# FFN of a two-layer DiT block: two elements at a time, first product as seven block products of 256 columns

## The chip, the cores and the metric

The kernel runs on one core of one Trainium2 chip. The metric is the device time of one execution in microseconds (us). A core has a matrix engine (TensorE, PE in the profile; PEld is its weight load), which writes only to PSUM, eight banks of 512 fp32 columns; VectorE (DVE) and ScalarE (ACT), which read and write PSUM and SBUF; GpSimd (POOL), which works on SBUF; and SyncE (SP), which here issues nearly all DMAs. Each engine works through its own queue, and semaphores order the queues.

## The reference

There are sixteen elements of 256 tokens by 256 channels, in fp32. Two layers follow each other; each is self attention, cross attention and a feed-forward network (FFN), every one preceded by a layer norm whose scale and shift are made from a condition vector ("modulation"), and followed by a residual sum. The change touches the two FFNs:

```python
h = _ln(x, ...) * (1 + scale) + shift        # per element, 256 x 256
g = gelu(h @ W1 + b1)                        # W1: 256 x 1024, exact gelu
x = x + g @ W2 + b2                          # W2: 1024 x 256
```

## The kernel before, in words

The work is cut into six phases (layer 0 self attention, cross attention, FFN; the same for layer 1), and each phase into sixteen jobs, one per element b (list `jobs`, from L840 on). A job has two steps in an attention phase and four in an FFN phase. The main loop goes through all steps; what is called in a step is written out by hand for each kind of phase. `manual_schedule` (L86) covers PE, DVE, ACT, POOL and SP: each of these engines executes its instructions in the order in which the program issues them, and there is no planner. In step s of job j the loop also works for neighbours: `prev` is j-1, `nxt` j+1, `after` j+2 and `third` j+3.

The input of a job takes this way. `prepare_moments` (L421) finds mean and variance on DVE and raises the variance to the power -0.5 on POOL. `prepare_norm` (L424) normalizes on DVE, transposes 32x32 blocks on DVE (`turn`, L352), writes them to DRAM with four DMAs on SP (`turned`), and adds the bias of the coming output to x on POOL (`add_bias`, L428). `prepare_fetch` (L444) reads them back transposed with four DMAs on SP (`fetched`). `prepare_input` (L449) applies scale and shift (`affine`, L402): the first 128 channels on ACT, the second on POOL, giving `hT`, channels by tokens, as two 128x256 blocks.

In an FFN job, step s calls `ffn_hidden` (L700): 2 of the 8 chunks of 128 hidden channels, each with two accumulated products over the 256 input channels, and a gelu of each chunk on ACT. `product` (L77) issues a 128x128 weight as four matmuls of 32 columns of the weight; the profile records two matmuls for each of these. So the hidden product of an element is 128 records of 256 columns. The output product of the element before runs in step 2 (`finish_folded`, L747): it is already a two-by-two block product with seven instead of eight multiplications; its operands are sums of blocks, made on DVE at step 0 (`fold_inner`, L738) for the activations and once per phase (`fold_weights`, L723) for the weights. It is 224 records of 128 columns. Five DVE additions then put the seven results into x. PSUM banks for an FFN are taken in rotation (`next_bank`, L73).

In the FFN jobs before the change the loop orders the calls so, beside hidden product and output product: moments and norm of `third` at step 1, fetch of `after` at step 1, input of `after` at step 3. In the first FFN phase three modulations for layer 1 are made: at step 3 of elements 2, 5 and 8 (L976) `modulation_turned` (L200) multiplies on TensorE, copies on ACT, transposes on DVE and issues sixteen small DMAs on SP (`turned_b`, L218); the scale and shift are computed from them at step 3 of elements 3, 6 and 9 (L949). At step 1 of element 3 the next phase's weights are loaded. In the second FFN phase, element 2 starts the load of all softmax sums back into SBUF (`look_outside`), and after step 3 of element 3 `judge` (L796) reduces them on DVE with two 128x2048 reductions.

At the start of an FFN phase the last attention job is still unfinished. In layer 0 its softmax sums are inverted in step 1 of element 0 (`sum_up`, L614, with DMAs on SP), its result is scaled on POOL at step 3 (`scale`, L631), and its output product runs at step 3 of element 1. In layer 1 its sums are inverted in step 0 of element 0 (`normalize`, L686: reciprocal and two shuffles on DVE, DMAs on SP, a multiplication on POOL) and its output product runs at step 2.

Of the kernel before, what the change touches and what calls it, by code (L numbers as in the profile page):

```python
# [10 lines left out]
F32 = mybir.dt.float32  # L11
I32 = mybir.dt.int32
AF = mybir.ActivationFunctionType
# [3 lines left out]
P = 128  # L17
# [26 lines left out]
def fast(ctx: ExitStack, tc: tile.TileContext, a: dict, out: bass.AP, flag):  # L44
# [6 lines left out]
    assert NB >= 11  # L51
# [25 lines left out]
    def product(out, lhsT, rhs, start, stop):  # L77


        for g in range(4):  # L80
            cut = slice(32 * g, 32 * g + 32)
            nc.tensor.matmul(out[cut], lhsT[:, cut], rhs, start=start, stop=stop)  # L82
# [239 lines left out]
    def zero_values():  # L322
        for i in range(2):
            wide_v.append(work.tile([P, NT, 8, 64], F32, tag="v", name=f"wide_v{i}"))
            nc.gpsimd.memset(wide_v[i], 1.0)
# [76 lines left out]
    def affine(pt, cw, scale, bias, tag, name, eng=nc.gpsimd):  # L402

        dst = work.tile([cw, 2, N], F32, tag=tag, name=name)
        nc.scalar.activation(dst[:, 0, :], pt[:, 0, :], AF.Identity, bias=bias(0), scale=scale(0))  # L405
        eng.tensor_scalar(dst[:, 1, :], pt[:, 1, :], scale(1), bias(1), ALU.mult, ALU.add)
        return dst
# [41 lines left out]
    def prepare_input(job):  # L449

        b, key = job["b"], job["key"]
        factor, addend = job["phase"]["mod"]
        job["hT"] = hT = affine(
            job.pop("hraw"), P,
            lambda c: factor[:, c, b : b + 1], lambda c: addend[:, c, b : b + 1], "hT", f"hT_{key}",
            nc.vector if b == 0 and job["p"] == 0 else nc.gpsimd,
        )
        if not job["cross"]:
            job["kT"] = hT
        elif job["layer"] == 0:  # L460
            job["kT"] = affine(
                job.pop("craw"), P,
                lambda c: column("L0_xcond_ca_lnc_w", c), lambda c: column("L0_xcond_ca_lnc_b", c),
                "cT", f"cT_{key}",
            )
# [23 lines left out]
    def layer1_values(job, at, t):  # L489
        w, kT = job["phase"]["w"], job["kT"]  # L490
        if t == 0:
            if not wide_v:
                zero_values()
            job["v"] = wide_v[job["index"] % 2]
# [227 lines left out]

    def fold_weights(ph):  # L723
# [3 lines left out]
        for m, x, y, op in ((1, b[0][0], b[1][1], ALU.add), (3, b[0][1], b[1][1], ALU.subtract),  # L727
                            (4, b[1][0], b[0][0], ALU.subtract), (6, b[0][0], b[0][1], ALU.add),
                            (7, b[1][0], b[1][1], ALU.add)):
            if ph["kind"] == "attn":  # L730
                folded[m] = wtile([P, 4, P], "folded", f"folded_w_{m}", 5)
            elif m == 7:
                folded[m] = work.tile([P, 4, P], F32, tag="cT", name=f"folded_w_{m}")
            else:
                folded[m] = work.tile([P, 4, P], F32, tag="qk", name=f"folded_w_{m}", bufs=4)
            (nc.gpsimd if ph["kind"] == "attn" else nc.vector).tensor_tensor(folded[m], x, y, op)
# [176 lines left out]
    for i, (j, s) in enumerate(steps):  # L913
# [40 lines left out]
        if ffn:  # L954
            ffn_hidden(job, s)
            if s == 1 and prev["kind"] == "attn" and layer0:
                sum_up(prev, next_bank())
            if s == 2 and prev["kind"] == "attn" and not layer0:
                finish(prev, next_bank())
            if prev["kind"] == "ffn":  # L960
                if s == 0:
                    fold_inner(prev, nc.vector, 5, 2, 1, 7, 6)
                if s == 2:
                    finish_folded(prev, (next_bank(), next_bank()))
            then = attention(i + 2, 1)
            if s == 2 and then:
                stage_a(then[0], 0, next_bank())
            if s == 0 and prev["kind"] == "attn" and prev["layer"] == 1:
                normalize(prev)
            if late is not None and s == 3:  # L970
                finish(late, next_bank())
            if s == 2 and then:
                for t in range(NT):
                    layer1_values(then[0], next_bank(), t)
            if make_mod:
                make_mod["mod"] = make_mod["make_mod"](next_bank())  # L976
            if s == 1 and after is not None:
                prepare_fetch(after)
            if s == 1 and third is not None:
                prepare_moments(third)  # L980
                prepare_norm(third)
            if s == 1 and prev["kind"] == "attn":
                fold_weights(job["phase"])
            if s == 3 and after is not None:
                prepare_input(after)
            if s == 3 and prev["kind"] == "attn" and layer0:
                scale(prev)
        elif layer0:
            then = attention(i + 1, 0)
            stage_t(job, 2 * s, 0)  # L990
# [32 lines left out]
            if s == 0:  # L1023
                prepare_moments(third)
                context_moments(third)
                prepare_fetch(after)
            else:
# [5 lines left out]
        else:  # L1033
# [16 lines left out]
            else:  # L1050
                prepare_norm(third)
                prepare_input(after)
        scores(i + 1)
# [4 lines left out]
    fold_inner(jobs[-1], nc.vector, 6, 5, 2, 1, 7)  # L1058
    finish_folded(jobs[-1], (1, 2, 3))
# [615 lines left out]
```

## Time and profile before

Three runs of the kernel took 2192.76 to 2195.17 us.

| | us |
|---|---|
| median of the runs shown | 2192.9 |
| profiled execution | 2193.98 |
| its span | 2192.2 |
| TensorE busy | 2175.6 |
| VectorE busy | 1663.5 |
| GpSimd busy | 1072.9 |
| ScalarE busy | 837.5 |
| first FFN phase, first to last of its matmuls | 1290.2 to 1505.4 |
| second FFN phase | 1974.7 to 2185.7 |

The first group of lines that the prediction shows is from the profile's page: busy time of each engine with its share of the span, busy tenths in 40 equal slices, and the shares of the engines in the chain of work that ended last. The second gives two stretches of the span and the busy time in each. The others are lines of the timeline: start, length, engine (SPq is SP's queue, issuing a DMA), line, operation, tile written and tiles read, shapes, count, and in brackets how long the engine stood idle before it and what ended that. Instructions that follow each other are merged into one line. The matmul ends are modelled, so a busy TensorE says that it had work in flight.

### The profile page before, as it was taken

Reading aid. Unit: us, or ns where it says so; the run is one execution under the profiler, and the core shown is the slowest. Engines: PE = TensorE matmul, PEld = TensorE weight load, DVE = VectorE, ACT = ScalarE, POOL = GpSimd, SP = SyncE. Lnnn points to the kernel's source line nnn. Section 1 sums busy time; section 2 is a strip of 40 time slices with the busy share of each in tenths; the row PEclk is TensorE's granted clock in tenths of the full one; section 3 lists DMA queues with packets and bytes.
Section 4 is the critical chain, followed back from the end, with each engine's and each line's share of the span. In section 5 each row is a group of like instructions: output and inputs, shape, how many; then the busy total and the mean of one; then the engine's idle time right before and its main releaser. Section 6 shows DMA issues by size and latency. Waiting matters only on the chain.

```text
span 2192.2 us, 110839 instructions
## 1 busy us (share of the span) xinstructions
PE 2175.6 (99%) x50504; PEld 1452.2 (66%) x50504; DVE 1663.5 (76%) x3121; ACT 837.5 (38%) x1308; POOL 1072.9 (49%) x1034
## 2 busy tenths in 40 slices
PE   9999999999999999999999999999999999999998
PEld 5656656656666666666666668887665555557898
DVE  6877777776888999989888876564777777777654
ACT  3323323323323332333333332233666666663222
POOL 3766566566657777676776752221322233222220
PEclk9999999999999999999999999999999999999999
DMA  6110110110132221212212033221212232223221
GB/s 192 49 37 23 26 38 23 27 38 22 29 86 69 71 62 35 58 42 45 56 36 61 23 74 87 43 56 27 65 40 42 56 94 57 62 52 86 61 63 37
DMA packets 309320, 117.83 MB, mean 54 GB/s; under 512 B 245652, under 2 KB 292072, under 8 KB 308712
## 3 DMA queue, kind: packets, MB, share of 16 engines
q1 hardware_dynamic: 308296, 110.12, 21.2%
q8 instruction: 397, 6.50, 1.3%
q14 instruction: 83, 0.68, 0.1%
q10 hardware_dynamic: 544, 0.52, 0.1%
HBM read 77.14 MB, written 33.29 MB: 50 GB/s over the span
## 4 chain that ended last, share of the span: by engine, by line
PE 90%; DVE 3%; POOL 2%; DMA 1%; issue 1%; SPq 1%; ACT 0%; DVEq 0%; POOLq 0%; ACTq 0%
PE banks L82 59%; PE banks L578 15%; PE banks L647 9%; PE banks L663 5%; PE banks L514 1%; PE banks L481 1%; DVE m L535 1%; POOL raw L636 1%; POOL qk L543 1%; POOL folded L745 0%; DMA spread<-sums_seen 0%; DMA sums_seen<-inv 0%; SPq L218 0%; DVE squares L605 0%; DVE rows L612 0%
## 5 line engine op out<-in xcount | busy, mean ns | idle before, releaser
L590 ACT ACTIVATE pr<-banks 128x1024 f32<-128x1024 f32 x576 | 487.5, 937 | 414.4 <-PE banks L578 211.0
L543 POOL TENSOR_TENSOR qk<-m,m 128x512 f32<-128x512 f32 x256 | 347.8, 1379 | 298.2 <-DVE m L535 203.9
L535 DVE TENSOR_TENSOR m<-banks,rope 128x512 f32<-128x512 f32 x512 | 324.0, 678 | 83.7 <-POOL qk L543 79.6
L599 DVE TENSOR_TENSOR both<-pr 128x512 f32<-128x512 f32 x256 | 222.3, 882 | 102.8 <-ACT pr L590 102.3
L654 ACT COPY raw<-banks 128x512 f32<-128x512 f32 x128 | 75.2, 587 | 465.7 <-PE banks L647 440.0
L578 PE MATMUL banks<-qk 32*64 32x256 f32 x8192 | 241.3, 378 | 3.6 <-DVE x L762 2.3
L647 PE MATMUL banks<-pr,v 128*32 128x256 f32 x4096 | 233.2, 379 | 0.0
L578 PEld LDWEIGHTS banks<-qk 32*64 32x64 f32 x8192 | 184.6, 131 | 64.4 <-issue 22.8
L713 ACT ACTIVATE g<-banks,cols 128x256 f32<-128x256 f32 x256 | 106.3, 471 | 273.7 <-PE banks L82 262.1
L647 PEld LDWEIGHTS banks<-pr,v 128*32 128x32 f32 x4096 | 132.9, 110 | 88.7 <-ACT pr L590 0.7
L82 PE MATMUL banks<-folded_w,folded 128*32 128x128 f32 x5856 | 177.8, 273 | 0.4 <-issue 0.4
L636 POOL TENSOR_TENSOR raw<-raw,spread 128x512 f32<-128x512 f32 x128 | 163.8, 1313 | 18.3 <-DMA spread<-sums_seen 16.1
L82 PEld LDWEIGHTS banks<-folded_w,folded 128*32 128x32 f32 x5856 | 166.2, 110 | 1.3 <-issue 0.9
L605 DVE STREAM_TRANSPOSE squares<-both 128x1024 f32<-128x1024 f32 x128 | 159.4, 1245 | 4.4
L612 DVE TENSOR_REDUCE rows<-squares 128x32 f32<-128x1024 f32 x128 | 155.4, 1214 | 2.2
L698 POOL TENSOR_TENSOR oT<-oT,spread 128x256 f32<-128x256 f32 x64 | 45.8, 736 | 210.0 <-DVE spread L697 210.0
L339 POOL TENSOR_TENSOR rstd<-ve,neg_half 128x2 f32<-128x2 f32 x95 | 74.3, 782 | 125.4 <-DVE ve L337 122.0
L663 PE MATMUL banks<-pr,wide_v 128*32 128x256 f32 x2048 | 134.4, 379 | 1.1 <-ACT pr L590 1.1
L82 PE MATMUL banks<-hT,wk_sa 128*32 128x256 f32 x2048 | 134.7, 381 | 0.5 <-ACT hT L405 0.5
L432 POOL TENSOR_TENSOR x<-x,bo_b 128x256 f32<-128x256 f32 x96 | 73.1, 782 | 125.9 <-DVE xh L347 125.9
L82 PE MATMUL banks<-hT,wq_ca 128*32 128x256 f32 x2048 | 133.9, 379 | 0.0
L82 PE MATMUL banks<-hT,wq_sa 128*32 128x256 f32 x2048 | 133.9, 379 | 0.0
(167 smaller groups left out, 3693.9 us busy)
## 6 DMA issues: line engine op xcount, KB each, us to landing
turned<-blocks SPq DMA_DIRECT2D x380, 64.0 KB
fetched<-turned SPq DMA_DIRECT2D x380, 64.0 KB
spread<-sums_seen SPq DMA_DIRECT2D x128, 128.0 KB
x<-in_x SPq DMA_DIRECT2D x16, 256.0 KB
fetched_c<-turned_c SPq DMA_DIRECT2D x64, 64.0 KB
cT<-in_ctx_turned SPq DMA_DIRECT2D x16, 256.0 KB
out<-x SPq DMA_DIRECT2D x16, 256.0 KB
ctx<-in_ctx SPq DMA_DIRECT2D x16, 192.0 KB
```

Source lines behind the costliest of these rows:

```text
L82: nc.tensor.matmul(out[cut], lhsT[:, cut], rhs, start=start, stop=stop)
L535: nc.vector.tensor_tensor(m, pq, rope[:, s : s + 1, :].to_broadcast([P, 2, N]), ALU.mult)
L543: nc.gpsimd.tensor_tensor(r, x, y, (ALU.subtract, ALU.add)[out])
L578: nc.tensor.matmul(banks[64 * g : 64 * g + 64, at + h, t * N : (t + 1) * N], lhs, rhs, start=(half == 0), stop=(half == 1 or job["layer"] ...
L590: nc.scalar.activation(pr[:, one], sc[:, one], AF.Exp, scale=0.125 if job["layer"] == 0 else 0.25)
L599: nc.vector.tensor_tensor(job["both"][:, 2 * p : 2 * p + 2, :], pr[:, :, 0, :], pr[:, :, 1, :], ALU.add)
L605: nc.vector.transpose(job["squares"].rearrange("p b k -> p (b k)"), job.pop("both").rearrange("p h n -> p (h n)"))
L612: nc.vector.tensor_reduce(job["rows"][:, u, :], job.pop("squares"), AX.X, ALU.add)
L636: nc.gpsimd.tensor_tensor(part, part, spread[:, u : u + 1, :].to_broadcast([P, 2, N]), ALU.mult)
L647: nc.tensor.matmul(o[32 * h : 32 * h + 32, half, :], v[:, t, col : col + 32], prs[h // 2][:, h % 2, t, :], start=(t == 0), stop=(t == NT - 1),
L663: nc.tensor.matmul(o[32 * h : 32 * h + 32], v[:, t, 4 * c + h, 32 * e : 32 * e + 32], prs[h // 2][:, h % 2, t, :], start=(t == 0), stop=(t ...
L713: nc.scalar.activation(g[:, c, :], ph[:, c, :], AF.Gelu, bias=column(w["b1"], 2 * u + c))
```

## The change

The FFN takes elements 0 to 13 in pairs (2n, 2n+1). The hidden product of a pair is a two-by-two block product: W1 cut into two halves of hidden channels and two of input channels, against the two 128-channel blocks of the two elements, 256 columns each. It is done in a form with seven block products M1 to M7, of which three results are built by adding onto a bank after an engine has read it. Each job does half of the hidden channels of both elements: step 0 issues M1, M6, M5 into three banks, ACT copies M1 out and DVE adds M6 to the copy; step 1 adds M2 onto M1's bank and M7 onto M6's, and DVE makes two more sums; step 2 adds M4 and M3 likewise, and DVE makes the last two. The weight sums are made on POOL before the phase (`fold_input_weights`); the sums of the inputs (`fold_input`) on POOL in step 1 of the odd job before the pair (on DVE for the first pair of the first FFN). The last two elements of each phase keep `ffn_hidden`.

The output product has the same form. Its activation folds move from DVE to POOL (`fold_hidden`) and it runs two jobs late instead of one: two of its seven products in step 1, five in step 3, followed by the additions into x. In the paired jobs the affine of `after` runs wholly on ACT and moves from step 3 to step 1, the fetch from step 1 to step 0, the norm from step 1 to step 2.

```diff
-    def product(out, lhsT, rhs, start, stop):
+    def product(out, lhsT, rhs, start, stop, **more):
...
-            nc.tensor.matmul(out[cut], lhsT[:, cut], rhs, start=start, stop=stop)
+            nc.tensor.matmul(out[cut], lhsT[:, cut], rhs, start=start, stop=stop, **more)
...
-        eng.tensor_scalar(dst[:, 1, :], pt[:, 1, :], scale(1), bias(1), ALU.mult, ALU.add)
+        if eng is nc.scalar:
+            nc.scalar.activation(dst[:, 1, :], pt[:, 1, :], AF.Identity, bias=bias(1), scale=scale(1))
+        else:
+            eng.tensor_scalar(dst[:, 1, :], pt[:, 1, :], scale(1), bias(1), ALU.mult, ALU.add)
...
+    def fold_input(pair, eng):
...
+        eng.tensor_tensor(t1, b[0][1], b[0][0], ALU.subtract)
+        eng.tensor_tensor(t2, b[1][1], t1, ALU.subtract)
+        eng.tensor_tensor(t3, b[1][1], b[0][1], ALU.subtract)
+        eng.tensor_tensor(t4, b[1][0], t2, ALU.subtract)
+        first["inner"] = second["inner"] = {1: b[0][0], 2: b[1][0], 3: b[1][1], 4: t4, 5: t1, 6: t2, 7: t3}
...
+    def block_products(job, out, m, start):
...
+        half = job["b"] % 2
+        for c in range(2):
+            at = (2 * half + c) * P
+            product(
+                out[:, c, :], job["phase"]["input_w"][m][:, at : at + P], job["inner"][m], start and c == 0, True,
+                skip_group_check=True,
+            )
+
+    def pair_hidden(job, pair, part):
...
+            block_products(job, x, 1, True)
+            block_products(job, y, 6, True)
+            block_products(job, z, 5, True)
+            nc.scalar.copy(copy, x)
+            nc.vector.tensor_tensor(six, y, copy, ALU.add)
...
+        if part == 1:
+            block_products(job, x, 2, False)
+            block_products(job, y, 7, False)
+            for c in range(2):
+                gelu(job, top[:, c, :], x[:, c, :], 2 * half + c)
+            nc.vector.tensor_tensor(seven, y, copy, ALU.add)
+            nc.vector.tensor_tensor(bottom2, z, seven, ALU.add)
+        else:
+            block_products(job, y, 4, False)
+            block_products(job, z, 3, False)
+            for c in range(2):
+                gelu(job, bottom2[:, c, :], bottom2[:, c, :], 4 + 2 * half + c)
+            nc.vector.tensor_tensor(bottom, y, copy, ALU.add)
+            nc.vector.tensor_tensor(top2, z, six, ALU.add)
...
-            if prev["kind"] == "ffn":
-                if s == 0:
-                    fold_inner(prev, nc.vector, 5, 2, 1, 7, 6)
-                if s == 2:
-                    finish_folded(prev, (next_bank(), next_bank()))
...
+            if s < 3 and paired:
+                pair_hidden(job, pair, s)
+            elif not paired:
+                ffn_hidden(job, s)
+            if s == 0:
+                if prev["kind"] == "attn" and not layer0:
+                    normalize(prev)
+                if after is not None:
+                    prepare_fetch(after)
+                if done is not None:
+                    fold_hidden(done, nc.gpsimd, 5, 6, 7, 3)
+            if s == 1:
+                if b == 0 and layer0:
+                    sum_up(prev, next_bank())
+                if third is not None:
+                    prepare_moments(third)
+                if done is not None:
+                    output_products(done, 1, 2)
+                if paired and after is not None:
+                    prepare_input(after, nc.scalar)
+                    if b % 2 == 1 and b < NB - 4:
+                        fold_input(jobs[j + 1 : j + 3], nc.gpsimd)
+                if b == 0:
+                    fold_output_weights(job["phase"], nc.vector)
...
+            if s == 2:
+                if third is not None:
+                    prepare_norm(third)
...
+            if s == 3:
+                if done is not None and b < NB - 1:
+                    output_products(done, 4, 5, 6, 7, 3)
+                    add_output(done, 5, 6, 7, 1, 2)
+                if late is not None:
+                    finish(late, next_bank())
+                if make_mod:
+                    make_mod["mod"] = make_mod["make_mod"](next_bank())
...
+            elif leaving and nxt["kind"] == "ffn":
+                prepare_input(after, nc.scalar)
+                fold_input((nxt, after), nc.vector)
+                prepare_norm(third)
...
+                if job["cross"] and job["b"] == 5:
+                    fold_input_weights(phases[job["p"] + 1], nc.gpsimd)
+                if nxt["kind"] == "ffn":
+                    fold_input((nxt, after), nc.gpsimd)
...
-    fold_inner(jobs[-1], nc.vector, 6, 5, 2, 1, 7)
-    finish_folded(jobs[-1], (1, 2, 3))
+    last = jobs[-1]
+    fold_hidden(last, nc.vector, 7, 5, 6, 3)
+    output_products(last, 1, 7, 2, 4, 5, 6, 3)
+    add_output(last, 7, 5, 6, 1, 2)
```

## The prediction, made before the change was run

> **What bounds the kernel now.** I read the busy lines and the 40 slices of the page first, then the chain that ended last, then the timeline of the two FFN phases, which the change rewrites, engine by engine. The busy line, the slices of PE and DVE, and the head of the chain:
>
> ```profile
> PE 2175.6 (99%) x50504; PEld 1452.2 (66%) x50504; DVE 1663.5 (76%) x3121; ACT 837.5 (38%) x1308; POOL 1072.9 (49%) x1034
> PE   9999999999999999999999999999999999999998
> DVE  6877777776888999989888876564777777777654
> PE 90%; DVE 3%; POOL 2%; DMA 1%; issue 1%; SPq 1%; ACT 0%; DVEq 0%; POOLq 0%; ACTq 0%
> ```
>
> TensorE is never idle for a whole slice and is 90% of the chain, so a matmul removed is time removed, and an idle microsecond put into TensorE's stream is a microsecond added. The same by windows: first FFN phase, second FFN phase, and the end of the program (columns: length, busy us of PE, PEld, DVE, ACT, POOL, granted clock, DMA):
>
> ```profile
> 1290.20:1505.40 215.20, 214.83 (x5667) 178.81 (x5659) 132.21 (x328) 61.26 (x145) 57.66 (x72) 1.00 0.28 61
> 1974.70:2185.70 211.00, 210.92 (x5672) 182.52 (x5662) 131.01 (x300) 60.79 (x143) 40.22 (x58) 1.00 0.26 62
> 2188.00:2192.00 4.00, 0.00 (x0) 0.00 (x0) 0.00 (x0) 0.00 (x0) 0.00 (x0) 0.82 0.15 43
> ```
>
> Both phases are full of matmuls. The timeline shows one element's first hidden matmul at 2164.49 and the next at 2177.51, so 13.02 us per element for 128 records of 256 columns and 224 of 128. By columns (61,440) that is 54.3 and 27.1 ns a record.
>
> The waits that matter later are on SP and ACT. In the first FFN phase, timeline of those two engines:
>
> ```profile
> 1332.10 11.54 SPq L218 DMA_DIRECT2D turned_b<-blocks_b  x16
> 1353.72 0.60 ACT L405 ACTIVATE hT<-fetched,add_a,fac_a 128x256 f32<-128x256 f32 x1 [8.69 <-DMA fetched<-turned]
> 1372.33 11.79 SPq L218 DMA_DIRECT2D turned_b<-blocks_b  x16
> 1384.22 1.91 SPq L372 DMA_DIRECT2D fetched<-turned  x4
> 1387.72 0.60 ACT L405 ACTIVATE hT<-fetched,add_a,fac_a 128x256 f32<-128x256 f32 x1 [2.46 <-DMA fetched<-turned]
> 1411.83 12.50 SPq L218 DMA_DIRECT2D turned_b<-blocks_b  x16
> ```
>
> Three times the sixteen small stores of a modulation keep SP for 11.5 to 12.5 us, the next element's fetch is issued right behind them (1384.12, then 1384.22), and ACT stands still until it lands. Today nobody minds: TensorE asks for that ACT result one or two elements later.
>
> **What the skill says.** The Trainium skill, "TensorE: Matmul & The Clock Gate", Architectural detail: ACT and DVE are strict first-in-first-out. The trace agrees: after the 8.69 us above six gelus follow back to back. "DMA: Bandwidth & Descriptors", Anatomy of one DMA: a semaphore wait of a DMA happens on the issuing sequencer. The fetch behind the stores agrees. "PSUM — Partial Sum Buffer", The four PSUM rules: a partial sum may be read, synchronised, in the middle of a group; nothing in this trace does so. "TensorE: Matmul & The Clock Gate" again, What's actually happening: an idle window of about 3.4 us halves the clock and one busy window restores it. The last window above shows a fall, mean 0.82 over 4 us: at half clock that is 1.4 us, so it began some 4.9 us after the last matmul (2185.67).
>
> **The change, part by part.**
>
> *Matmuls removed.* A pair's hidden product had 256 records of 256 columns; fourteen block products of 16 leave 224. 32 x 54.3 ns = 1.74 us per pair, seven pairs, two phases: **-24.3 us**. The output product keeps seven products of 32 records. One block product and one output product each take 0.87 us, so an element becomes 14 x 0.87 = 12.15 us.
>
> *Steady state.* DVE per element: five sums from PSUM (0.69, as the 128x512 row of the residual add: 3.4), moments 1.24, normalizing and turning 1.45, five residual adds 0.42 to 0.69 with their dependences 2.8; total 8.9 to 9.4 of 12.15. POOL: four folds at 1.29 to 1.42 (its rows in attention) 5.4, two bias adds 1.52, a power 0.7, half of the pair's four 128x256 sums at 0.76, 1.5: 9.1. ACT: eight gelus 3.4 (two in 0.84), copy 0.59, both affine halves 1.23: 5.2. All fit behind 12.15; the tightest is the first PSUM sum, which waits for the previous residual adds until about 2.3 us into the element and must be done by 3.5. Cover gone, every late microsecond there is TensorE's. I cost it at 0.
>
> *The new coupling.* The order is what costs. TensorE now adds M2 onto the bank that ACT must copy first, and M7 and M4 onto a bank that DVE must read first. On ACT, the copy of element e+1 is queued behind six gelus of e, and those behind the affine of element e+2, moved from the last step to the second. That affine waits for a fetch on SP.
>
> Ordinary element: the turn ends at 10.3 us, its four stores issue in 2.7 and land 3.1 later (gaps of 3.2 in the trace), the fetch issues in 1.75 and lands 1.7 later: 19.6, which is 7.4 in the next element. Affine 1.2, six gelus 2.6: 11.3; the next copy is due at about 13.0. Covered, with 1.7 us to spare.
>
> *Elements 3, 6, 9 of the first FFN phase.* The sixteen stores start about 2.5 us into them (after the residual adds) and the fetch is queued behind: 2.5 + 11.7 = 14.2, fetch and landing 17.6, affine 18.9, gelus 21.4, copy 22.0. TensorE is through the element at 12.15 plus 0.4 to 0.85 for the modulation. After 6 it needs the copy at 15.4: 6.7 us idle. After 3 and 9 a new pair begins, whose M6 needs t2, that is affine (18.9) and two sums on POOL (1.6): 20.4, where M1 ended at 13.7: 6.7. Three times: **+20.1 us**.
>
> *Entry of the first FFN phase (first matmul 1290.2).* DVE's residual add ends at 1291.5, then come the pair's four sums at 0.42 and the normalizing of element 2. M6 waits 1.5; the first sum and the next then hold M7 0.4 and M4 0.8. Element 2's turn ends at 1294.7 (1292.8 today), its fetch lands at 1303.9, so affine, six gelus and copy end at 18.1 us after entry; TensorE needs that copy at 11.5: 6.9 with signals. Then M4 1.0, and the last attention output waits 1.3 for POOL's scaling, whose sums are also behind that fetch on SP. Sum **+11.9**.
>
> *Entry of the second (1974.7).* The timeline before, DVE and POOL:
>
> ```profile
> 1976.08 1.53 POOL L432 TENSOR_TENSOR x<-x,bo_b 128x256 f32<-128x256 f32 x2 [2.77 <-DVE xh L347]
> 1976.93 1.71 DVE L689 RECIPROCAL sums<-sums 128x256 f32<-128x256 f32 x1
> 1977.59 0.56 POOL L406 TENSOR_SCALAR hT<-fetched,fac_b,add_b 128x256 f32<-128x256 f32 x1
> ```
>
> The pair's sums queue on POOL behind these: 1978.15 + 2 x 0.76 = 1979.7, where M1 ends at 1975.6: 4.15. The reciprocal and two shuffles (2.6) stand before the second PSUM sum: M4 waits 1.7. The fetch of element 2 is behind that reciprocal's stores: copy late by 2.9, M4 by 1.0. Elements 0 and 1 have no output product to fill time, so element 3's affine and the sums of pair (2,3) are late for M6: 5.4. Sum **+15.2**.
>
> *The judging reductions.* Two 128x2048 reductions, 2.28 us each, plus two comparisons, stand on DVE after element 3 of the second phase, between its residual adds and the first PSUM sum of element 4. Spare is 0.5 of 4.9: **+4.4**.
>
> *Small.* The last residual adds after the last product are 0.72 + 0.58 where one of 0.42 stood: **+0.7**. Weight folds: one fewer per FFN; the input folds run on POOL under the last attention products (POOL idles 6.99 us before 1291.9). Value tiles' fill moves within POOL's spare time: 0. Slowed clock: five idles above are longer than 4.9 us, each at most 1.7 us of lost work (half of that page's 3.4, an estimate); 0 to 8.5, I take **+3**.
>
> Sum: -24.3 + 20.1 + 11.9 + 15.2 + 4.4 + 0.7 + 3.0 = **+31.0** on the profiled execution's 2193.98 (span 2192.2): 2225. The median shown is 1.1 lower, so **2224 us**, 1.4% slower. The waits follow from laying rows end to end in queue order and might each be off by a third: 2203 to 2245.
>
> **The rivals.**
>
> *Faster: the affine holds no one.* The fetch is now issued a step earlier, and if it lands before ACT comes to it, M2 finds its copy. Then the 20.1, the 6.9 and 2.9 at the entries and the 5.4 vanish, with the slow clock: 31.0 - 35.3 - 3 = -7.3: **2186 us**. For it: ordinary elements fit by my own count. Against: the three fetches behind sixteen stores are on record. It decides at 28 us of these 35: only if four fifths go is the kernel no slower. 14%.
>
> *Between.* One large group (the modulations, or both entries) is hidden and the rest stays: 2190 to 2203. 8%.
>
> *VectorE becomes the bound.* With POOL folding all through, the 128x512 sums could take 30% longer: 9.4 becomes 12.2, above 12.15, and the first sum comes about 1 us late in each of 28 elements: **2252 us**. Against: with POOL busy in attention, the 128x512 multiplications from PSUM still take 678 ns. 6%.
>
> *The saving does not come.* If weight loads set the pace, fewer columns would buy nothing; but records are dropped whole, load and all, and both shapes run at one rate per column. I give it no share of its own.
>
> **How the numbers follow.** 72% for the likeliest (2203 to 2245; 2224), 8, 14 and 6 for the rest. The range 2190 to 2245 leaves out the faster rival and VectorE's, that is 20%. About 0.2% (4.4 us) is what a measurement of this kernel can tell from no change. Faster takes its rival's 14%, same 4% from the low end of the middle case, slower 82%.
>
> **What would show it.** FFN matmul records fall by 14 x 32 = 448. In the first FFN phase TensorE idles about 6.7 us three times, some 44 us apart, released by ACT's copy or POOL's sum, with ACT waiting for the fetch just before; the phases last 235 and 218 us against 215.2 and 211.0. The prediction is wrong if the affine never waits more than about 4 us in either phase, if M6 of the second phase starts within 1 us of M1's end, or if the elements in between differ from 12.15 us.

## The result and the profile after

The changed kernel takes 2231.7 us (median of four runs, 2230.5 to 2232.9) where the kernel before, run beside it, takes 2192.8 (2191.9 to 2195.2): ratio 1.0176, 95% interval 1.0158 to 1.0193, that is 1.8% slower. The forecast was 2224, slower, with a range to 2245. The profiled execution took 2232.9 us, its span is 2231.1. One execution of the kernel with the stores spread, below, took 4554.2 us and is left out of its times.

From the page of the changed kernel: busy line, slices of TensorE and of its granted clock, shares of the chain that ended last.

```profile
PE 2169.1 (97%) x50056; PEld 1414.1 (63%) x50056; DVE 1682.7 (75%) x3120; ACT 868.8 (39%) x1365; POOL 1238.3 (56%) x1177
PE   9999999999999999999999988799999999998998
PEclk9999999999999999999999999899999999999999
PE 88%; DVE 5%; SPq 2%; POOL 2%; DMA 1%; issue 1%; ACT 1%; DVEq 0%; POOLq 0%; ACTq 0%
```

The saving came as forecast: 50504 - 50056 = 448 records fewer. But TensorE now has four more slices that are not full, three in the first FFN phase (one of them with a lower clock) and one in the second, and busy time fell by 6.5 us only, where 448 records are worth 24.3. Slow matmuls count as busy: part of the saving was paid back in longer records.

The two FFN phases by windows, each from its first matmul to the next phase's first one or the last matmul (columns as in the prediction: length; busy us of PE, PEld, DVE, ACT, POOL; granted clock; DMA). First before, then after:

```profile
1290.18:1499.92 209.74, 209.37 (x5567) 175.11 (x5563) 129.46 (x322) 61.26 (x145) 57.66 (x72) 1.00 0.28 62
1974.74:2185.67 210.93, 210.88 (x5670) 182.52 (x5662) 130.94 (x300) 60.75 (x143) 40.22 (x58) 1.00 0.26 62
```

```profile
1289.40:1528.24 238.84, 207.91 (x5345) 154.61 (x5340) 140.88 (x325) 77.51 (x173) 130.80 (x138) 0.94 0.23 53
2002.64:2223.71 221.07, 205.66 (x5446) 163.80 (x5438) 140.46 (x295) 77.07 (x171) 122.14 (x128) 0.97 0.24 59
```

The first phase is 29.1 us longer, the second 10.1; the attention between them is 474.8 before and 474.4 after, and the end after the last matmul grew from 6.5 to 7.4. With the start of the first FFN 0.8 earlier that is the whole difference of the spans, 38.9. The forecast was 19.8 longer for the first (235 against 215.2) and 7.0 for the second (218 against 211.0).

The waits of TensorE after (what it waited for: us in total, times, longest):

```profile
PE banks L82 <- POOL inner L751: 22.6, 4, 7.8
PE banks L82 <- ACT sums L782: 14.5, 3, 7.2
PE banks L82 <- DVE sums L783: 3.9, 1, 3.9
PE banks L82 <- DVE sums L803: 3.3, 4, 0.9
PE banks L82 <- DVE inner L751: 1.9, 1, 1.9
```

None of these rows was there before. `inner` is a pair's input sum on GpSimd, `sums L782` the copy on ACT, `L783` and `L803` the PSUM sums on VectorE. Together 46.2 us (51.6 forecast). By place, from the timeline: behind the modulations 6.97, 7.17 and 7.76 (21.9), entry of the first phase 1.88, 0.74, 5.59 and 0.81 (9.0), entry of the second 3.88, 0.91, 1.75, 0.81 and 3.99 (11.3), judging 3.94. So the ledger of the two phases is +39.2 = -24.3 + 46.2 + 17.3, and the last term, which my sum had at 3, is worked out below, from one experiment and from the record of the clock.

The queue that I named, in the timelines of ACT and SP after:

```profile
1336.76 11.44 SPq L218 DMA_DIRECT2D turned_b<-blocks_b  x16
1348.30 2.63 SPq L372 DMA_DIRECT2D fetched<-turned  x4
...
1352.60 0.60 ACT L405 ACTIVATE hT<-fetched,add_a,fac_a 128x256 f32<-128x256 f32 x1 [13.35 <-DMA fetched<-turned]
```

and what TensorE does meanwhile:

```profile
1346.86 1.04 PE L82 MATMUL banks<-hT,w_a 128*32 128x256 f32 x16
1354.87 3.64 PE L82 MATMUL banks<-inner,put_w_L_xcond_ff_b 128*32 128x256 f32 x32 [6.97 <-POOL inner L751]
1358.28 1.69 PE L82 MATMUL banks<-hT,w_a 128*32 128x256 f32 x16
1359.80 1.04 PE L82 MATMUL banks<-inner,put_w_L_xcond_ff_b 128*32 128x256 f32 x16
```

The fetch is issued when the sixteen stores are out, ACT stands 13.35 us for it, and block product 6 of element 4 comes 6.97 us after block product 1 is through. Then M6 and M5, two block products, take 3.64 us where a pair of them takes 1.9 elsewhere, and M2 1.69 where it takes 1.04.

### The profile page after: what moved, and what is told of

Same layout as the page of the kernel before. It is cut to its first block, busy times and chain, and to the rows that moved or that the text cites. A ratio compares the mean times of both kernels' runs of the same rounds, so it can differ in the third digit from the quotient of the medians.

```text
span 2231.1 us, 110154 instructions
## 1 busy us (share of the span) xinstructions
PE 2169.1 (97%) x50056; PEld 1414.1 (63%) x50056; DVE 1682.7 (75%) x3120; ACT 868.8 (39%) x1365; POOL 1238.3 (56%) x1177
## 4 chain that ended last, share of the span: by engine, by line
PE 88%; DVE 5%; SPq 2%; POOL 2%; DMA 1%; issue 1%; ACT 1%; DVEq 0%; POOLq 0%; ACTq 0%
PE banks L82 57%; PE banks L582 15%; PE banks L651 9%; PE banks L667 5%; SPq L218 1%; PE banks L518 1%; PE banks L485 1%; DVE m L539 1%; DVE x L868 1%; POOL raw L640 1%; DVE rows L616 0%; DVE both L603 0%; DVE squares L609 0%; DMA fetched<-turned 0%; POOL qk L547 0%
## 5 line engine op out<-in xcount | busy, mean ns | idle before, releaser
L640 POOL TENSOR_TENSOR raw<-raw,spread 128x512 f32<-128x512 f32 x128 | 162.3, 1303 | 21.3 <-DMA spread<-sums_seen 20.1
L868 DVE TENSOR_TENSOR x<-banks,x 128x256 f32<-128x256 f32 (+2 forms) x155 | 82.3, 531 | 68.7 <-PE banks L82 62.1
L582 PE MATMUL banks<-q,k 32*64 32x256 f32 x4096 | 128.3, 381 | 0.4 <-ACT g L717 0.4
L889 POOL TENSOR_TENSOR folded<-raw,raw 128x512 f32<-128x512 f32 x90 | 127.1, 1440 | 2.4
```

The source lines that it names most:

```text
L582: nc.tensor.matmul(banks[64 * g : 64 * g + 64, at + h, t * N : (t + 1) * N], lhs, rhs, start=(half == 0), stop=(half == 1 or job["layer"] ...
L640: nc.gpsimd.tensor_tensor(part, part, spread[:, u : u + 1, :].to_broadcast([P, 2, N]), ALU.mult)
L889: eng.tensor_tensor(folded[m], *sums[m])
```

## The experiments

My theory: fetches and DMAs late on SP hold ACT and GpSimd, and TensorE, whose bank is now added onto, waits for them; the sum of my steps is the loss. The rivals on record: the affine holds no one; VectorE is the bound. A further one came up with the ledger: a clock term several times what I gave it. Each run changes the changed kernel; only the moved factors build on the spread stores, and the last two runs each on the run before. Beside these runs the kernel before took 2193.0 to 2194.3 us, so a difference of 1 to 2 us between two of them tells nothing.

**All hidden products single.** The plain product for all sixteen elements; the new output product, the moved norms and fetches stay. The sums for the pairs fall away too, and the affine goes back to step 3, half of it on GpSimd, because it hangs on the same condition. Do pairs cost what they lost?

```diff
-            paired = b < NB - 2
+            paired = False
```

> All sixteen elements take the plain hidden product (eight products), everything else of the change stays: output product in the new form, two elements late, folds on GpSimd, norm and fetch moved. TensorE gets 24.3 us of work back. Theory: the idles (46.2) and the slow clock (15.5) hang on the coupled sums and go: 2231.7 + 24.3 - 61.7 = 2194 us, the time of before within 4. Rival (the rest of the change costs): 2205 to 2256 us.

Measured: 2203.9 us, ratio 1.0044 (1.0029 to 1.0058). The pairs, which remove 24.3 us of matmuls, cost 27.8 us: their coupling, with the moved affine, is worth some 52. The rest of the change is not free, as I had expected it to be: 10 us over the kernel before. Its waits name most of it:

```profile
PE banks L82 <- DVE x L871: 4.0, 3, 2.1
PE banks L82 <- POOL raw L640: 3.3, 2, 3.1
```

4.0 us are residual adds late behind the modulation's factors on VectorE, 3.3 the scaling of the late attention, whose sums now queue on SP behind a fetch (the longest, 3.13 us, is followed by 3.4 us of half clock, 1.7 of them lost); some 1 us is the longer end.

**The stores of the modulations spread.** Up to six of a modulation's sixteen stores are issued behind the fetch of each of the next three elements, and the factors are computed three elements later.

```diff
-                nc.sync.dma_start(
-                    out=turned[32 * q : 32 * q + 32, g // KC, g % KC, :], in_=blocks[32 * g : 32 * g + 32, q, 0:NB]
-                )
+                waiting_stores.append((store, q, g))
...
-        if ffn and layer0 and job["b"] in (3, 6, 9) and s == 3:
+        if ffn and layer0 and job["b"] in (6, 9, 12) and s == 3:
...
                     prepare_fetch(after)
+                some_stores(6)
```

> Theory (late ScalarE): the affine of the element after next waits on ScalarE for a fetch that stands behind sixteen stores on SP, and TensorE waits for the copy or the pair's sums behind it; each idle then lets the clock fall. Here the sixteen stores go six at a time behind the fetches of the next three elements. The three idles of 7.0, 7.2 and 7.8 us and their slow clock (2.3 + 2.1 + 1.7) go: 2231.7 - 28 = 2204 us, up to 2208 if the weight loads of element 3 hold something up. Rival (the coupling itself: adding onto a bank that ScalarE or VectorE has read, and GpSimd's folds, cost a little in every element): no change, 2230 or more.

Measured: 2213.7 us (2212.2 to 2216.5), ratio 1.0097 (1.0076 to 1.0117): 18 us less, not 28. In the profiled execution the first phase is 16.4 us shorter. The old idles are gone, and with them ACT's wait. But after elements 6, 9 and 12 stand new ones of 3.93, 2.83 and 3.43 us, released by the first PSUM sum on VectorE. The timelines of VectorE and GpSimd in this run:

```profile
1379.87 0.73 DVE L175 TENSOR_TENSOR add_b<-turned_b,cols 128x32 f32<-128x32 f32 x1
1380.63 1.21 DVE L176 SCALAR_TENSOR_TENSOR fac_b<-add_b,cols 128x32 f32<-128x32 f32 x1
1381.88 1.32 DVE L177 SCALAR_TENSOR_TENSOR add_b<-add_b,cols 128x32 f32<-128x32 f32 x1
1383.23 1.20 DVE L178 TENSOR_TENSOR add_b<-add_b,cols 128x32 f32<-128x32 f32 x1
1384.47 1.19 DVE L179 TENSOR_TENSOR add_b<-turned_b,add_b 128x32 f32<-128x32 f32 x1
...
1380.51 1.28 POOL L849 TENSOR_TENSOR folded<-g 128x512 f32<-128x512 f32 x1
1381.87 1.28 POOL L849 TENSOR_TENSOR folded<-folded,g 128x512 f32<-128x512 f32 x1
```

Five operations of 32 columns, 0.19 us each in the changed kernel (1396.69 to 1397.79 there), take 5.7 us, and each ends with an operation of GpSimd, the first with a bias add, the others with a fold: 1380.63 + 1.21 = 1381.84 against 1380.51 + 1.28 = 1381.79; 1381.88 + 1.32 = 1383.20 against 1381.87 + 1.28 = 1383.15. The Trainium skill, "SBUF — State Buffer", Who interferes with whom, says that a VectorE instruction with two SBUF inputs contends with a GpSimd instruction that reads SBUF. The trace agrees: the ends fall together within 0.05 us.

**The factors moved.** The stores spread as above; the five operations come after the first PSUM sum of elements 7, 10 and 13.

```diff
-        if ffn and layer0 and job["b"] in (6, 9, 12) and s == 3:
-            at = phases[1 + job["b"] // 3]
-            at["mod"] = at["mod"]()
...
                 pair_hidden(job, pair, s)
+            if layer0 and b in (7, 10, 13) and s == 0:
+                at = phases[1 + b // 3]
+                at["mod"] = at["mod"]()
```

> The stores of the three modulations are spread as before (six behind the fetch of each of the next three elements), and the five small VectorE operations that turn the landed product into factors now come after the first PSUM sum of elements 7, 10 and 13 instead of ahead of the residual adds of elements 6, 9 and 12. Theory: they took 0.73 to 1.32 us each there because GpSimd was at its folds in the same moments; in the new place GpSimd stands still, they take 0.19 us each as in the changed kernel (1.1 us in a gap of 2 us), and the three idles go with their slow clock: 2231.7 - 21.9 (idles) - 6.1 (slow clock after them) = 2204 us, give or take 2. Rival: the operations are slow because they read what a DMA has just written, whoever works beside them: 5.7 us in a gap of 2 us again, three idles of 2.5 to 4 us, 2213 to 2217 us.

Measured: 2203.65 us, ratio 1.0045 (1.0028 to 1.0061). That is the 28 us: the first phase takes 209.9 us, where the changed kernel's takes 238.8 and that of before 209.7. VectorE and GpSimd in the same place:

```profile
1385.27 0.18 DVE L175 TENSOR_TENSOR add_b<-turned_b,cols 128x32 f32<-128x32 f32 x1
1385.49 1.20 DVE L176 SCALAR_TENSOR_TENSOR fac_b<-add_b,cols 128x32 f32<-128x32 f32 x1
1386.73 0.19 DVE L177 SCALAR_TENSOR_TENSOR add_b<-add_b,cols 128x32 f32<-128x32 f32 x1
...
1385.37 1.28 POOL L849 TENSOR_TENSOR folded<-g,folded 128x512 f32<-128x512 f32 x1
```

GpSimd's last fold lies over the second operation alone, which ends with it (1386.69 and 1386.65); the others take 0.19. Freshly written inputs are no cause: the first one reads what the DMA wrote and takes 0.18, and 0.19 in the changed kernel, where it starts as the DMA lands (1396.69).

**The even element's affine one element later.** ACT no longer meets that fetch in element 6.

```diff
-                if paired and after is not None:
+                if paired and after is not None and b % 2 == 1:
+                    prepare_input(nxt, nc.scalar)
                     prepare_input(after, nc.scalar)
-                    if b % 2 == 1 and b < NB - 4:
+                    if b < NB - 4:
```

> The affine of an even element is done one element later, next to that of the odd one, when the pair's sums need it; stores as in the change. Theory: ScalarE is not held in even elements, so the idle of 7.2 us after element 6 with 2.1 of slow clock, the one of 5.6 us with 3.3 at the first entry and one of 1.8 us at the second go: 2212 us; the idles before M6 of elements 4 and 10 stay at 7 to 8 us, that of element 2 in the second phase at 4 to 5.5. Rival: no change, 2230 or more.

Measured: 2228.8 us, ratio 1.0155 (1.0138 to 1.0172), a miss: 2212 was expected. ACT now copies in time (1389.99), yet the idle of element 7 shrinks only from 7.17 to 5.19 and moves behind a VectorE sum. VectorE, then TensorE, in this run:

```profile
1392.91 0.19 DVE L175 TENSOR_TENSOR add_b<-turned_b,cols 128x32 f32<-128x32 f32 x1 [6.14 <-DMA turned_b<-blocks_b]
1394.19 2.86 DVE L868 TENSOR_TENSOR x<-banks,x 128x256 f32<-128x256 f32 x5 [0.17 <-issue]
1397.70 1.94 PE L82 MATMUL banks<-inner,put_w_L_xcond_ff_b 128*32 128x256 f32 x16 [5.19 <-DVE sums L783]
```

The stores hold two queues. VectorE stands for their landing with the factors, ahead of the residual adds and the next PSUM sum, and was only 2.3 us less late than ACT. In the changed kernel the same wait is there (5.54 us, to 1396.69), hidden behind ACT's. The first entry shows the same: its idle of 5.59 us shrinks to 2.82 only, since the gelus ahead of ACT's copy now wait 3.50 us for a VectorE sum that stands behind the moments and the output weights' folds.

**The judging late.** `judge` after element 14, its count within element 15.

```diff
...
-        if job["last"] and s == 3 and job["b"] == 3:
+        if job["last"] and s == 3 and job["b"] == 14:
             judge(*seen_sums)
+        if job["last"] and s == 2 and job["b"] == 15:
+            count_outside()
```

> The two judging reductions are moved from behind element 3 to behind element 14 of the second FFN phase, where no PSUM sum follows. Theory: one idle of 3.9 us and 2.7 us of slow clock go: 2225 us. Rival (VectorE is short of time all through): they cost the same elsewhere, 2231 to 2232 us.

Measured: 2225.5 us, ratio 1.0141 (1.0125 to 1.0158): 6.2 us less, for an idle of 3.94. The rest, 2.3 us, is slow clock: the second phase takes 6.2 us less (214.9 against 221.1).

**The idles of the modulations filled.** Six more block products in each of the three places; nothing else moves.

```diff
             block_products(job, x, 1, True)
+            if job["layer"] == 0 and job["b"] in (4, 10):
+                for _ in range(6):
+                    block_products(job, y, 1, True)
...
+            if job["layer"] == 0 and job["b"] == 7:
+                for _ in range(6):
+                    block_products(job, bank((turn_of_ffn[0] + 1) % 8, 2, N), 1, True)
```

> The changed kernel, with six more block products (6 x 0.87 = 5.2 us of matmuls whose result is written over and not used) put into each of the three idles behind the modulations (ahead of block product 6 of elements 4 and 10, ahead of block product 2 of element 7). Nothing else starts earlier or later. Theory: the slow clock after an idle is lost time of its own, 2.3 + 2.1 + 1.7 = 6.1 us in these three places; kept busy, TensorE keeps its clock: 2231.7 - 6.1 = 2225.6 us, give or take 1. Rival: the wait ends when ACT and GpSimd are ready, and the slow stretch is made up for by later slack: 2231.7 us, no change.

Measured: 2222.6 us (2220.3 to 2225.4), ratio 1.0136 (1.0119 to 1.0153): 9.1 us less with 15.6 us of matmuls more. Element 4 takes 21.64 us without filling (1346.86 to 1368.50), which is 12.15 + 6.97 + 2.52; filled it takes 19.75 = 12.15 + 5.20 of filling + 2.20 of idle + 0.20. Element 7: 21.57 and 19.70. There the slow clock was lost time. Element 10 gains nothing (21.77 and 21.76): the clock fell to half all the same, at 1443.0, after an idle of 2.54 us. So the three places give 3.8 us of the 6.1 expected, and the rest of the 9.1 did not come from the filling. Of the 10.8 us between the two profiled spans 2.6 lie in elements 0 and 1, and 4.3 in the second phase, where the two kernels are the same. The judging there, after and filled (timeline of TensorE):

```profile
2064.09 1.93 PE L82 MATMUL banks<-inner,input_w_L_xcond_b 128*32 128x256 f32 x16 [3.94 <-DVE sums L783]
2065.77 3.67 PE L82 MATMUL banks<-w_b,g 128*32 128x128 f32 x64
```

```profile
2055.92 1.07 PE L82 MATMUL banks<-inner,input_w_L_xcond_b 128*32 128x256 f32 x16 [3.94 <-DVE sums L789]
2056.78 1.96 PE L82 MATMUL banks<-w_b,g 128*32 128x128 f32 x64
```

The same idle to a hundredth, once followed by half speed and once not. The granted clock in the traces shows why. In the changed kernel it falls at 1304.97, 1352.76, 1400.55, 1444.92, 2008.12, 2032.01 and 2062.73 us. The distances are 14, 14, 13, 165, 7 and 9 times 3.413 us, and each slow stretch is one, two or three times as long. Some of the stretches by windows (length; busy us of TensorE; granted clock; DMA), with the sum of all seven:

```profile
1304.98:1315.22 10.24, 7.09 (x68) 0.50 0.39 94
1352.76:1359.59 6.83, 4.72 (x48) 0.50 0.74 214
...
2032.02:2035.43 3.41, 3.41 (x36) 0.50 0.31 79
2062.73:2069.56 6.83, 5.47 (x84) 0.50 0.00 0
sum 44.38, PE 31.69; mean PE 4.53
```

In every other execution with more than one fall they lie on such a grid too, set off differently. What TensorE worked in the step of the grid just ahead decides. The step ahead of the fall at judging; then, in the filled kernel, the two steps that share the same idle, neither followed by a fall, and the step ahead of the fall at 1443.0:

```profile
2059.32:2062.73 3.41, 0.83 (x16) 1.00 0.47 154
```

```profile
2050.57:2053.99 3.42, 1.41 (x28) 1.00 0.44 122
2053.99:2057.40 3.41, 1.48 (x40) 1.00 0.18 52
1439.59:1443.00 3.41, 0.95 (x20) 1.00 0.40 63
```

Over all twelve profiled executions, up to the last matmul and without the first 20 us, the clock fell after every step in which TensorE was busy for less than 0.39 of the time, and after none in which it was busy for more than 0.41. "TensorE: Matmul & The Clock Gate", What's actually happening, says that the clock is judged in windows of about 3.4 us that run freely, and halves after an idle one. The length and the free run agree with the 3.413 us; that the window must be wholly idle does not, and the measurement decides. As an estimate from these figures, one idle of up to 2.0 us (0.6 of a step) does not halve the clock by itself, one above 4.1 us (twice that) always does, and between them it depends on where the idle falls.

**GpSimd's order before the second phase.** The pair's sums go ahead of the bias adds of element 2.

```diff
+            elif nxt["kind"] == "ffn":
+                prepare_input(after)
+                fold_input((nxt, after), nc.gpsimd)
+                prepare_norm(third)
             else:
```

> The changed kernel, but before the second FFN phase GpSimd gets the second half of element 1's affine and the first pair's four sums ahead of the bias adds of element 2. Theory of the prediction (block product 6 waits for what stands before those sums on GpSimd): rows of the changed kernel give 0.55 + 2 x 0.76 from 2001.2 us, so sum t2 is there when block product 1 ends at 2003.7; the idle of 3.88 us and the 1.7 us of slow clock after it go: 2231.7 - 5.6 = 2226 us, give or take 1. Rival: what the first wait gives back the copy of element 1 asks for (its fetch comes no earlier), 2229 to 2231 us.

Measured: 2227.5 us, ratio 1.0157 (1.0140 to 1.0174), 4.2 us less, between the two expectations: both had a part. Block product 6 follows block product 1 without a pause (2002.22, 2003.09), as theory had it. But M4 of that element waits 1.98 instead of 0.91 and the copy of element 1 3.72 instead of 1.75, because the reciprocal and the fetch behind it come no sooner; the M6 of pair (2, 3) waits 1.29 instead of 3.99.

**A mended kernel.** Pairs from element 2 to 13 only, with what the runs showed: stores spread, factors moved, judging late, the late attention's sums ahead of a fetch, two output products of element 0 ahead of block product 6 of element 2, VectorE's weight folds later, and the last product's order changed so that fewer adds stand at the end.

```diff
-            paired = b < NB - 2
+            paired = 2 <= b < NB - 2
...
                 if b == 0 and layer0:
                     sum_up(prev, next_bank())
+                    prepare_fetch(after)
...
-    output_products(last, 1, 7, 2, 4, 5, 6, 3)
+    output_products(last, 1, 2, 7, 5, 6, 4, 3)
```

> A version with what the runs point to: pairs from element 2 to 13 only (elements 0, 1, 14, 15 one at a time), stores spread and factors moved as above, the judging reductions at elements 14 and 15, the weight folds of element 0 behind the turn of element 3, the late attention's sums ahead of the fetch of element 2, output products 1 and 2 of element 0 ahead of block product 6 of element 2, and the last output product's order changed. If the waits found are all there is, the matmuls decide: 12 pairs' worth at 1.74 us less (6 per phase, 20.9 us) against the kernel before, 2192.8 - 20.9, plus 1 to 4 us for what is left at the entries and the end: 2173 to 2176 us. If the cost of the kernel with single hidden products (2203.9) stays in it, 2203.9 - 20.9 = 2183 us.

Measured: 2180.6 us, ratio 0.9943 (0.9927 to 0.9960): faster than the kernel before, but short of the 2173 to 2176 that held if the waits found were all; 2183 was expected if the cost of the kernel with single products stayed. An idle of 3.60 us is left ahead of M6 of element 2 in the second phase, with 1.5 us lost to the slow clock, and 1.6 us at the late attention.

**Mended further, first.** The stores of the last normalizing go behind the fetch of element 2 and the turn of element 3; the late attention's sums are taken a step sooner.

> The mended kernel with two moves more. At the second FFN phase the four stores of the last normalizing (read again only by the judging) go behind the fetch of element 2 and the turn of element 3, which they held up by 2.8 us: the idle of 3.6 us ahead of block product 6 of element 2 falls to about 0.8, and the 1.7 us of slow clock after it go. At the first, the late attention's sums are taken after the first instead of the second part of element 0: its idle of 1.6 us goes. Expected: 2180.6 - 2.8 - 1.7 - 1.6 = 2174.5 us, give or take 1.5. Rival: the fetch of element 3 waits for its own turn and not for the queue, then only the 1.6 us go: 2179 us.

```diff
-                    normalize(prev)
+                    normalize(prev, False)
...
+                if b == 0 and not layer0:
+                    prev["stores"]()
```

Measured: 2180.9 us, ratio 0.9937 (0.9924 to 0.9951). A miss, close to the rival. The turn of element 3 was issued 2.9 us sooner in its phase, but its fetch only 1.1 sooner (it waits for the turn to land) and took 2.84 us to issue instead of 2.30; 3.03 of the 3.60 us are still there.

**Mended further, second.** The output product of element 0, folded early on VectorE, fills that idle.

> The second mended kernel still idles 3.0 us ahead of block product 6 of element 2 in the second FFN phase and then works 1.6 us at the slow clock: the fetch of element 3 waits for its own turn to land. Here the output product of element 0 fills that place: VectorE, idle from 1982 to 1990 us, folds its four operands at the end of element 1, and six of its seven products (5.2 us, no work added) come ahead of block product 6. Expected: 2180.9 - 3.0 - 1.6 = 2176.3 us, give or take 1.5. Rival: the wait ends when GpSimd's sums are there, and the matmuls moved ahead are missing later, between block products 7 and 4 (0.9 us) and behind the residual adds: 2178 to 2180 us.

```diff
-                output_products(done, 1, 2)
+                output_products(done, *((1, 2) if job["layer"] == 0 else (1, 2, 4, 5, 6, 7)))
...
+                    if b == 1 and not layer0:
+                        fold_hidden(prev, nc.vector, 5, 6, 7, 3)
```

Measured: 2179.1 us, ratio 0.9929 (0.9916 to 0.9943). 2176.3 was expected: the idle is gone, but part of it stands one element later (1.28 us at 2001.50), and the time is in the rival's range. Waits of TensorE, and the two phases by windows:

```profile
PE banks L82 <- ACT sums L804: 2.3, 2, 1.3
...
PE banks L82 <- POOL raw L652: 1.3, 4, 0.8
```

```profile
1291.72:1494.93 203.21, 200.23 (x5377) 162.21 (x5372) 134.95 (x310) 73.42 (x168) 131.79 (x140) 1.00 0.28 63
1969.14:2172.00 202.86, 200.87 (x5478) 158.99 (x5470) 137.13 (x290) 73.29 (x167) 115.53 (x122) 1.00 0.27 65
```

Twelve pairs are worth 20.9 us of matmuls; the phases are 6.5 and 8.1 shorter than before, 14.6 together, at full clock. The three mended kernels cannot be ranked by their intervals; all three beat both kernels.

## Why the prediction was right, and where it was not

None of the three signs of being wrong appeared: the affine waited 13.35 us, M6 of the second phase 3.88, and ordinary elements took 12.16.

*Matmuls, -24.3.* Right: 448 records, and an ordinary element takes 12.16 us (1334.70 to 1346.86), so steady state costs nothing.

*Three modulations, +20.1.* 21.9, in the three places and behind the ACT wait named. But the step was half told: I listed ACT's queue behind the stores and not VectorE's, though the factors are computed right there. The even element's late affine showed it: freeing one queue uncovers the other. Spreading the stores and moving the factors took the 28 us away.

*Entry of the first phase, +11.9.* 9.0. M6 1.88 for 1.5, M4 0.74 for 0.8, the copy 5.59 for 6.9, the next M4 0.81 for 1.0. M7's 0.4 and the late attention's 1.3 did not come: they lay in the other waits' shadow.

*Entry of the second, +15.2.* 11.3: M6 3.88 for 4.15; M4 0.91 for 1.7, since VectorE's reciprocal and shuffles, behind the first sum, ended 0.6 us before M7 did; copy 1.75 for 2.9; M4 0.81 for 1.0; M6 of pair (2, 3) 3.99 for 5.4. Later waits are shorter than a sum of steps laid end to end, because each earlier idle gives them time. Taking M6's wait away showed it from the other side: 5.6 us expected, 4.2 won.

*Judging, +4.4.* 3.94, and 6.2 with what its removal won. *End, +0.7.* 0.9.

*Slowed clock, +3.* This is the term that was mis-sized, by far: 17.3 us remain in the ledger of the two phases. The windows above name most of them: TensorE worked 31.69 us at half clock, of which half, 15.8 us, is lost. That is five times my figure and above the bound of 8.5 that I had put on it. Thirteen restarts of TensorE after a wait, at some 0.17 us each (the record's end against the next start in an unbroken stream), are another 2.2; the two sum to 18.0, 0.7 more than the ledger has. Two things failed in that step. I bounded the loss by 1.7 us an idle, half of one window, where a slow stretch lasted up to three: the first entry lost 3.5, element 4 2.4 and judging 2.7. And I counted idles above 4.9 us only, the delay read at the program's end. That delay depends on where the idle begins on the grid: it was 2.6 us at judging, and idles of 3.88 to 3.99 us halved the clock three times in this execution.

The waits were 5.4 us too high, the clock with the restarts 14 too low, and the earlier start and the attention took 1.2 back: 2231.7 instead of 2224. That the central figure is this near is in part luck, since the two errors have opposite signs.

*The rivals.* That the affine holds no one is refuted by the 13.35 us above. VectorE is not the bound: elements without a modulation keep 12.16 us. Its sum was also wrong, since 30% more on the 3.4 us of large sums makes 9.4 into 10.4 and not 12.2. Neither middle case happened. A contention of VectorE with GpSimd exists, but not where I had put it: the large sums read PSUM and kept 0.69 us; small operations with both inputs in SBUF were stretched from 0.19 to 1.2 us. One reading proved less than I said: the fetch behind the stores shows the order of the queue. That a fetch's wait for its data holds the issuing queue is shown by SP's own waits, 83.8 us for landing turns in the kernel before.

## What to carry to other kernels

When an addition onto a bank in PSUM waits for an engine to have read it, every queue in front of that reader becomes TensorE's queue: list for each late DMA all engines that wait for it, not the one that is latest today. Cost an idle of TensorE of more than about 2 us with a risk of half speed on top: seven idles of 3.9 to 7.8 us lost 1.7 to 3.5 us each here. A saving in matmuls that is spread over a phase can be kept by leaving the ends of the phase, where the pipeline is not yet filled, in the old form: with twelve pairs instead of fourteen and the queues in order the same idea won 0.7% where it had lost 1.8%. No run tried the twelve pairs without the other changes, so their share in this is not shown.

## What was unexpected of the hardware

The same idle of 3.94 us was followed by half clock in one execution and by full clock in another, and one of 2.54 us was followed by half clock. The clock changed only on a grid of 3.413 us, and fell where TensorE had worked less than about 0.4 of the step before; a slow stretch lasted one to three steps (6.8 us around the idle of 6.97, 3.4 from 1443.0 in the filled kernel). A VectorE operation of 32 columns with two inputs in SBUF took 1.2 us when it met a 1.28 us fold of GpSimd, and 0.19 otherwise.
